# Layer 1 of the last sample: its 81 taps as diagonal matmuls in 64x64 tiles, in three lanes beside layer 2

## The chip, the core and the metric

The kernel runs on one core of a Trainium2 chip. The metric is the device time of one execution in microseconds (us), the median of several runs. Engines are named as in the profile: PE is TensorE (PEld its weight loads), DVE is VectorE, ACT is ScalarE, POOL is GpSimd, SP is the engine that only issues DMAs here.

## The reference: what is computed

Four layers with residuals work on x of shape (4, 256, 48, 48), fp32; each takes a group norm of x (32 groups) as its input.

```python
x = x + L0(gn(x))   # 8-head attention over all 2304 positions, then a 256x512 projection
x = x + L1(gn(x))   # a gate per channel: max pool, blur, 81-tap depthwise convolution, sigmoid
x = x + L2(gn(x))   # non-local block: attention with 64 channels, projection, batch norm
x = x + L3(gn(x))   # channel attention, 3x3 depthwise convolution, instance norm, leaky relu
```

Layer 1 is the one that is changed, for sample 3 alone:

```python
x_tem = blur_pool(max_pool_3x3(x), stride=3)               # 48x48 -> 16x16, per channel
x_h1 = dwconv(x_tem, w_h1, ((5, 5), (1, 1)))               # 11x3
x_w1 = dwconv(x_tem, w_v1, ((1, 1), (5, 5)))               # 3x11
x_h2 = inv_h(dwconv(h_transform(x_tem), w_h2, ...))        # 11x3 along a diagonal
x_w2 = inv_v(dwconv(v_transform(x_tem), w_v2, ...))        # 3x11 along the other
s = x_h1 + x_w1 + x_h2 + x_w2
gate = sigmoid((s - bn_mean) * bn_gamma / sqrt(bn_var + eps) + bn_beta)
return x * nearest_upsample(gate)
```

The four depthwise kernels fall on 81 different shifts of a 13x13 grid, so s is a sum of 81 shifted 16x16 images, each times one weight per channel.

## The kernel before: the parts that matter here

256 channels lie as two halves k = 0, 1 on 128 partitions. The main loop, `attend`, records attention in groups of two key blocks. In each group it issues the scores of this group, the pairwise sums for the softmax denominator of the group before, whatever else is due (`fills`), one step of the generators in `others`, and the value products of the group before. All engines run in program order (`manual_schedule`); only semaphores tie them together.

```python
for t, (u, g, st) in enumerate(groups):
    for j in range(g * G, (g + 1) * G):
        scores(u, j)                # 4 matmuls 64x64 tiles (fp32), then ACT: pt = exp(...)
    if prev is not None:
        add_up(*prev)               # POOL: half = pt0 + pt1;  DVE: acc += half
    do(due, t)
    do(fills, t)
    ...                             # lanes: next(gen) when due; a yielded number is the wait in groups
    if prev is not None:
        for j in ...: weigh(pu, j)  # value matmuls, 64x64 tiles
```

There are 16 phases of layer 0 (54 groups each) and then 4 phases of layer 2 (27 groups each). In layer 0 four of nine groups of a unit send their sum to POOL (`PAIRED`), in layer 2 of samples 0 to 2 all nine do. A query chunk ends with a total:

```python
def total(u):
    ab = [pj_tile()[:, :SL] for _ in range(2)]
    ...                                                # ones-matmuls over u["acc"]
    row = hpool.tile([P, 2, SL], F32, tag="half", name="row")   # hpool has 3 buffers
    for i in range(2):
        nc.scalar.copy(row[:, i, :], ab[i])
    ...                                                # l6 <- row by DMA, inverted, broadcast
```

Layer 1 of samples 0 to 2 runs beside layer 0 of the next sample. That of sample 3 runs beside layer 2 of samples 0 to 2, and the projection of sample 3 for layer 2 (`project2`) can only follow it. Its taps:

```python
def strips(b, k, norm, res):
    pd = lp.tile([P, 28, 28], F32, tag="pd", name="pd")
    nc.gpsimd.memset(pd, 0.0)
    blur = ...
    for half in range(2):
        ...                       # 12 ticks of DVE: maxima and blur of x, in tiles t1, t2, t3
    nc.scalar.activation(pd[:, 6:22, 6:22], blur, AF.Identity, bias=norm["nb"][...], scale=rs64)

    def products(n):              # 4 taps a round (5 in the first), 81 in all
        for i, t in enumerate(ROUNDS[n]):
            dr, dc = TAPS[t]
            nc.scalar.activation(
                bufs[n % 3][:, :, min(n, 1) + i].rearrange("p (r c) -> p r c", c=AS),
                pd[:, PAD + dr : PAD + dr + AS, PAD + dc : PAD + dc + AS],
                AF.Identity, scale=grid[:, k, g : g + 1],
            )
    ...
        nc.vector.tensor_reduce(to, bufs[n % 3][:, :, : min(n, 1) + len(taps)], AX.X, ALU.add)
```

and how sample 3 was placed:

```python
l1 = [l1_all(b) for b in range(B)]       # gn, strips 0, strips 1 with gated 0 aside, gated 1, gn
...
fns = project2(b + 1, norms2[b + 1], twos[b + 1])
if b + 2 == B:
    slots = list(range(n - 6, n))        # sample 3's projection: the last 6 groups of sample 2
spread(work, fns, slots)
...
others.append((part(l1[B - 1], ticks, b + 2 == B), ticks, first, end))
```

`gated` multiplies x by the gate (POOL, three strips of 128x768) and adds the constant part (DVE, three strips); `w_stats` multiplies a finished part of layer 2's result by W into two `pj` tiles and takes their statistics on DVE. All of `pj`'s users share two PSUM tiles.

Of the kernel before, what the change touches and what calls it, by code (L numbers as in the profile page):

```python
# [14 lines left out]
P = 128  # L15
# [59 lines left out]
def usual_path(  # L75
# [32 lines left out]
    load_x(0)  # L108
    vec = cpool.tile([P, 9, NK], F32, name="vec")
    nc.scalar.dma_start(vec, vecs)  # L110
    dw = cpool.tile([P, 4, NK, 33], F32, name="dw")
    nc.scalar.dma_start(dw, dww)

    wtp = thphi_w.rearrange("(k p) o -> p k o", p=P)
    w2c = cpool.tile([P, NK, 3, D], F32, name="w2c")
# [47 lines left out]
    def rsqrt(o, i):  # L163
        nc.gpsimd.tensor_tensor(o, i, mhalf[:, : i.shape[1]], ALU.pow)
# [5 lines left out]
    def gn(b, res, halves=range(NK)):  # L170

        if "st" not in res:
            res["st"] = small.tile([P, NK, NSL, 6], F32, tag="gn_st", name="gn_st")
        st = res["st"]
        for s in range(NSL):
            for k in halves:
                nc.vector.bn_stats(st[:, k, s, :], X[b][:, k, s * SL : (s + 1) * SL])
            yield 0
        mv = small.tile([P, NK, 2], F32, tag="gn_mv", name="gn_mv")
        for k in range(NK):  # L180
            nc.vector.bn_aggr(mv[:, k, :], st[:, k].rearrange("p s f -> p (s f)"))
        yield 3
        ps = pj_tile()
        nc.tensor.matmul(ps[:, 0:NK], lhsT=gmat, rhs=mv[:, :, 0], start=True, stop=True)
        gm = small.tile([P, NK], F32, tag="gn_gm", name="gn_gm")
        nc.vector.tensor_copy(gm, ps[:, 0:NK])
        dev = small.tile([P, NK], F32, tag="gn_dev", name="gn_dev")
        nc.vector.tensor_sub(dev, mv[:, :, 0], gm)
        sq = small.tile([P, NK], F32, tag="gn_sq", name="gn_sq")
        nc.vector.tensor_mul(sq, dev, dev)  # L190
        nc.vector.tensor_add(sq, sq, mv[:, :, 1])
        yield 2
        ps = pj_tile()
        nc.tensor.matmul(ps[:, 0:NK], lhsT=gmat, rhs=sq, start=True, stop=True)
        gv = small.tile([P, NK], F32, tag="gn_gv", name="gn_gv")
        nc.vector.tensor_scalar(gv, ps[:, 0:NK], GN_EPS, None, ALU.add)
        rs = small.tile([P, NK], F32, tag="gn_rs", name="gn_rs", bufs=6)
        rsqrt(rs, gv)
        yield 2
        nb = small.tile([P, NK], F32, tag="gn_nb", name="gn_nb", bufs=6)  # L200
        nc.vector.scalar_tensor_tensor(nb, gm, -1.0, rs, ALU.mult, ALU.mult)
        res["rs"], res["nb"] = rs, nb
        yield 1
# [82 lines left out]
    def total(u):  # L286

        ab = [pj_tile()[:, :SL] for _ in range(2)]
        for h, c in enumerate(HALVES):
            for r, out in zip(HALVES, ab):  # L290
                nc.tensor.matmul(  # L291
                    out[c], lhsT=ones[r], rhs=u["acc"][r, h, :], start=True, stop=True
                )
        row = hpool.tile([P, 2, SL], F32, tag="half", name="row")
        for i in range(2):
            nc.scalar.copy(row[:, i, :], ab[i])
        u["l6"] = small.tile([P, 2, LW], F32, tag="l6", name="l6")
        for c in HALVES:
            for i in range(2):
                nc.sync.dma_start(  # L300
                    u["l6"][c, i, :],
                    row[c.start : c.start + 1, i, :].rearrange("o (p w) -> o p w", w=LW),
                )

    def invert(u):
# [270 lines left out]
        }  # L576


    grid = lp.tile([P, NK, GRID * GRID], F32, name="grid")
    nc.gpsimd.memset(grid, 0.0)  # L580
    g2 = grid.rearrange("p k (r c) -> p k r c", r=GRID)
    for k in range(NK):
        wh1 = dw[:, 0, k, :].rearrange("p (a b) -> p a b", b=3)
        wv1 = dw[:, 1, k, :].rearrange("p (a b) -> p a b", b=11)
        wh2 = dw[:, 2, k, :].rearrange("p (a b) -> p a b", b=3)
        wv2 = dw[:, 3, k, :].rearrange("p (a b) -> p a b", b=11)
        s = g2[:, k, 1:12, 5:8]
        nc.gpsimd.tensor_add(s, s, wh1)
        s = g2[:, k, 5:8, 1:12]
        nc.gpsimd.tensor_add(s, s, wv1)  # L590

        s = grid[:, k, 23 : 23 + 132].rearrange("p (a t) -> p a t", t=12)[:, :, 0:3]
        nc.gpsimd.tensor_add(s, s, wh2)

        for a in range(3):
            s = grid[:, k, 11 + 13 * a : 11 + 13 * a + 132]
            s = s.rearrange("p (b t) -> p b t", t=12)[:, :, 0]
            nc.gpsimd.tensor_add(s, s, wv2[:, a, :])
    inv1 = lp.tile([P, NK], F32, name="inv1")
    v1 = lp.tile([P, NK], F32, name="v1")  # L600
    nc.vector.tensor_scalar(v1, vec[:, V_V1, :], BN_EPS, None, ALU.add)
    rsqrt(inv1, v1)
    nc.vector.tensor_mul(inv1, inv1, vec[:, V_G1, :])

    NT = 4
    ROUNDS = [range(0, NT + 1)] + [
# [3 lines left out]
    STRIP_TICKS = 2 * 6 + 2 + len(ROUNDS)  # L610
    GATE_TICKS = 7

    def strips(b, k, norm, res):

        xb = X[b][:, k, :].rearrange("p (r c) -> p r c", c=HW)
        pd = lp.tile([P, AS + 2 * PAD, AS + 2 * PAD], F32, tag="pd", name="pd")
        nc.gpsimd.memset(pd, 0.0)
        blur = lp.tile([P, AS, AS], F32, tag="blur", name="blur")
        for half in range(2):

            r0, nr = ((0, 25), (22, 26))[half]
# [40 lines left out]
            )  # L662
            yield half

        rs64 = lp.tile([P, 1], F32, tag="rs64", name="rs64")
        nc.vector.tensor_scalar(rs64, norm["rs"][:, k : k + 1], 1.0 / 64.0, None, ALU.mult)
        nc.scalar.activation(
            pd[:, PAD : PAD + AS, PAD : PAD + AS], blur, AF.Identity,
            bias=norm["nb"][:, k : k + 1], scale=rs64,
        )  # L670

        bufs = [
            lp.tile([P, L1_BUF], F32, tag=tag, name="prod").rearrange("p (n s) -> p n s", s=NT + 1)
# [3 lines left out]
        def products(n):  # L677
            for i, t in enumerate(ROUNDS[n]):
                dr, dc = TAPS[t]
                g = (dr + 6) * GRID + dc + 6  # L680
                nc.scalar.activation(  # L681
                    bufs[n % 3][:, :, min(n, 1) + i].rearrange("p (r c) -> p r c", c=AS),
                    pd[:, PAD + dr : PAD + dr + AS, PAD + dc : PAD + dc + AS],
                    AF.Identity, scale=grid[:, k, g : g + 1],
                )

        products(0)
# [3 lines left out]
        for n, taps in enumerate(ROUNDS):  # L691
            last = n == len(ROUNDS) - 1
            if n + 2 < len(ROUNDS):
                products(n + 2)
            to = bufs[(n + 1) % 3][:, :, 0]
            if last:
                res["acc"] = lp.tile([P, AS, AS], F32, tag="l1acc", name="l1acc")
                to = res["acc"].rearrange("p r c -> p (r c)")
            nc.vector.tensor_reduce(  # L699
                to, bufs[n % 3][:, :, : min(n, 1) + len(taps)], AX.X, ALU.add  # L700
            )
            yield 0

    def gated(b, k, norm, res):

# [169 lines left out]
    def l1_all(b):  # L875
# [20 lines left out]
        yield from gated(b, 1, norms1[b], one)  # L896
        yield from gn(b, norms2[b], [1])

    L1_ALL = 2 * GN_TICKS + NK * STRIP_TICKS + GATE_TICKS
    l1 = [l1_all(b) for b in range(B)]  # L900

    def part(gen, n, last):
        while n > 0 or last:
            wait = next(gen, None)
            if wait is None:
                return
            n -= 1
            yield wait

    def spread(work, fns, slots):  # L910

# [18 lines left out]
    for i, (b, p) in enumerate(order):  # L930
# [15 lines left out]
        if (b, p) == (2, 0):  # L946
            for s in range(NSL):
                work.setdefault(s, []).append(lambda s=s: send(s))
                work.setdefault(s + 8, []).append(lambda s=s: receive(s))
        if b > 0:  # L950
            ticks = -(-L1_ALL // NPAIR)
            first = AT_AFTER + 2 if p == 0 else 0
            others.append((part(l1[b - 1], ticks, p == NPAIR - 1), ticks, first, n - 2))
        if (b, p) == (B - 1, NPAIR - 1):
            others.append((part(l1[b], L1_AHEAD, False), L1_AHEAD, n - L1_AHEAD - 3, n))
        if p == 1 and b + 1 < B:
            others.append((gn(b + 1, norms0[b + 1]), GN_TICKS, 0, n - 2))
        phases.append(([l0_unit(b, p, c, pairs[b][p]) for c in range(NCH)], work, others))
# [2 lines left out]
    for b in range(B):  # L961
# [8 lines left out]
        if b + 1 < B:  # L970
            spread(work, stats(b, 0), [23, 24])
            fns = project2(b + 1, norms2[b + 1], twos[b + 1])
            slots = [s for s in range(n) if s % NG not in (2, 3, 4, 5, 6)]
            if b + 2 == B:
                slots = list(range(n - 6, n))
            spread(work, fns, slots)
            first, end = 4 if b == 0 else 0, n - 6 if b + 2 == B else n
            ticks = (L1_ALL - L1_AHEAD) * (end - first) // (3 * n - 6 - 4) + 1
            others.append((part(l1[B - 1], ticks, b + 2 == B), ticks, first, end))
        else:  # L980
            spread(work, stats(b, 0), [14, 15])
            spread(work, stats(b, 1), [23, 24])
            others.append((diagonals(), NK * len(PE_TAPS), 4, 22))
# [1232 lines left out]
```

## Time and profile before

| | before |
|---|---|
| median of 3 runs | 3762.78 us (3761.7 to 3763.52) |
| span of the profiled execution | 3765.1 us |
| scores, PE | 13,824 matmuls 64x384 in layer 0, 1,728 in layer 2 |
| exponentials, ACT | 1944, 814 ns each |
| pair sums `half`, POOL | 477, 1957 ns each |
| taps of layer 1, ACT | 648, 371.5 us in all four samples |
| reductions of taps, DVE | 152, 1480 ns each |

How to read it: an instruction stands as line, engine, operation, out<-in, shape and count; an fp32 matmul appears as two passes. The rows by stretch give for each engine the busy time and the number of instructions, then the granted share of the TensorE clock, the DMA share and GB/s. Layer 2's first scores with the tiles `qv`, `kd` start at 3014.9 us; the first tap of the last sample's layer 1 is at 3104.2 us, its last at 3304.0 us.

### The profile page before, as it was taken

Reading aid. Unit: us, or ns where it says so; the run is one execution under the profiler, and the core shown is the slowest. Engines: PE = TensorE matmul, PEld = TensorE weight load, DVE = VectorE, ACT = ScalarE, POOL = GpSimd, SP = SyncE. Lnnn points to the kernel's source line nnn. Section 1 sums busy time; section 2 is a strip of 40 time slices with the busy share of each in tenths; the row PEclk is TensorE's granted clock in tenths of the full one; section 3 lists DMA queues with packets and bytes.
Section 4 is the critical chain, followed back from the end, with each engine's and each line's share of the span. In section 5 each row is a group of like instructions: output and inputs, shape, how many; then the busy total and the mean of one; then the engine's idle time right before and its main releaser. Section 6 shows DMA issues by size and latency. Waiting matters only on the chain.

```text
span 3765.1 us, 85621 instructions
## 1 busy us (share of the span) xinstructions
PE 3547.9 (94%) x35954; PEld 1761.9 (47%) x35954; DVE 2544.2 (68%) x3199; ACT 2395.9 (64%) x3865; POOL 1354.2 (36%) x858
## 2 busy tenths in 40 slices
PE   7999999999999999999999999999999988789685
PEld 4454545555444445444444444444444543345343
DVE  2455545458778675587786756777867567866687
ACT  4656666565876875558768755587686548754353
POOL 1333333333334233333333433333333354564242
PEclk9999999999999999999999999999999998899897
DMA  3111111111111111311111111111111100000001
GB/s 134 25 25 21 26 22 25 21 27 18 28 17 25 21 29 16 79 16 29 16 29 16 29 16 30 15 29 17 29 12 25 18 4 6 5 6 6 26 30 72
DMA packets 114748, 97.84 MB, mean 26 GB/s; under 512 B 56384, under 2 KB 111792, under 8 KB 112560
## 3 DMA queue, kind: packets, MB, share of 16 engines
q1 hardware_dynamic: 111584, 91.14, 13.2%
q8 instruction: 283, 4.64, 0.5%
q10 hardware_dynamic: 2768, 1.14, 0.1%
q14 instruction: 113, 0.93, 0.1%
HBM read 59.33 MB, written 11.80 MB: 19 GB/s over the span
## 4 chain that ended last, share of the span: by engine, by line
PE 70%; DVE 18%; ACT 6%; issue 3%; POOL 2%; DMA 1%; DVEq 0%; SPq 0%; ACTq 0%; POOLq 0%
PE sc L238 26%; PE av L258 26%; DVE acc L284 6%; PE pj L499 6%; PE pj L556 4%; PE pj L513 3%; ACT prod L681 3%; DVE sc L1206 2%; PE pj L291 1%; ACT pt L244 1%; DVE av L1206 1%; PE pj L775 1%; DVE acc L278 1%; PE pj L803 1%; POOL half L269 1%
## 5 line engine op out<-in xcount | busy, mean ns | idle before, releaser
L244 ACT ACTIVATE pt<-sc 128x768 f32<-128x768 f32 x1944 | 1478.4, 814 | 947.0 <-PE sc L238 944.5
L269 POOL TENSOR_TENSOR half<-pt 128x768 f32<-128x768 f32 x477 | 933.2, 1957 | 1764.1 <-ACT pt L244 1656.9
L238 PE MATMUL sc<-q,k 64*64 64x384 f32 x13824 | 1290.2, 486 | 20.4 <-DVE q L544 11.2
L258 PE MATMUL av<-pt,v 64*64 64x384 f32 x13824 | 1291.7, 486 | 0.0
L284 DVE TENSOR_TENSOR acc<-acc,pt 128x768 f32<-128x768 f32 x792 | 863.9, 1091 | 105.8 <-ACT pt L244 24.3
L238 PEld LDWEIGHTS sc<-q,k 64*64 64x64 f32 x13824 | 521.8, 133 | 640.1 <-issue 514.0
L258 PEld LDWEIGHTS av<-pt,v 64*64 64x64 f32 x13824 | 524.1, 133 | 602.8 <-issue 567.2
L284 DVE TENSOR_TENSOR acc<-acc,half 128x768 f32<-128x768 f32 x459 | 480.0, 1046 | 289.7 <-POOL half L269 288.0
L560 DVE SCALAR_TENSOR_TENSOR x<-pj,bo,x 128x384 f32<-128x384 f32 x192 | 117.7, 617 | 409.7 <-PE pj L556 408.9
L681 ACT ACTIVATE prod<-pd,grid 128x256 f32<-128x256 f32 x648 | 371.5, 750 | 0.7 <-DVE prod L699 0.5
L499 PE MATMUL pj<-xs,w 128*128 128x384 f32 x768 | 265.2, 489 | 0.0
L699 DVE TENSOR_REDUCE prod<-prod 128x256 f32<-128x1280 f32 x152 | 224.9, 1480 | 29.6 <-ACT prod L681 29.1
L335 POOL TENSOR_TENSOR o<-o,rinv 128x384 f32<-128x384 f32 x95 | 117.8, 1240 | 344.7 <-DMA rinv<-rinv 331.6
L238 PE MATMUL sc<-qv,kd 64*64 64x384 f32 x1728 | 174.3, 508 | 40.3 <-ACT pt L244 40.2
L556 PE MATMUL pj<-o,wo 128*128 128x384 f32 x384 | 163.9, 525 | 21.6 <-DVE bias L466 10.9
L499 PEld LDWEIGHTS pj<-xs,w 128*128 128x128 f32 x768 | 139.2, 192 | 77.4 <-ACT v L518 4.8
L258 PE MATMUL av<-pt,qv 64*64 64x384 f32 x1728 | 175.1, 509 | 0.0
L513 PEld LDWEIGHTS pj<-w,xs 128*128 128x128 f32 x1152 | 137.5, 193 | 56.9 <-issue 50.9
L513 PE MATMUL pj<-w,xs 128*128 128x128 f32 x1152 | 155.0, 285 | 1.6 <-ACT w L468 1.6
L278 DVE TENSOR_TENSOR acc<-pt 128x768 f32<-128x768 f32 x99 | 122.5, 1237 | 24.3 <-ACT pt L244 24.3
L238 PEld LDWEIGHTS sc<-qv,kd 64*64 64x64 f32 x1728 | 72.3, 139 | 119.8 <-ACT pt L244 58.0
L327 ACT COPY raw<-av 128x768 f32<-128x768 f32 x108 | 86.2, 799 | 39.5 <-PE av L258 39.5
(216 smaller groups left out, 2547.1 us busy)
## 6 DMA issues: line engine op xcount, KB each, us to landing
xs<-in_x_dram SPq DMA_DIRECT2D x96, 384.0 KB
rinv<-rinv SPq DMA_DIRECT2D x208, 94.5 KB
x<-in_x_dram SPq DMA_DIRECT2D x6, 1152.0 KB
out_dram<-x SPq DMA_DIRECT2D x6, 1152.0 KB
l<-row SPq DMA_DIRECT2D x416, 1.5 KB
w<-in_wqkv_dram SPq DMA_DIRECT2D x32, 192.0 KB
rinv<-ls SPq DMA_DIRECT2D x208, 1.5 KB
x_out<-x SPq DMA_DIRECT2D x6, 384.0 KB
```

The lines of the kernel that those rows point to most:

```text
L238: nc.tensor.matmul(ps[c * D : (c + 1) * D, h, :SL], lhsT=u["of"]["k"][r, j0 : j0 + D], rhs=u["of"]["q"][r, u["qc"]], start=True, stop=True,)
L244: nc.scalar.activation(pt, ps[:, :, :SL], AF.Exp, scale=u["scale"])
L258: nc.tensor.matmul(u["av"][h * D : (h + 1) * D, half, :SL], lhsT=value(u, j, h)[r], rhs=pt[r, h, :], start=j == 0, stop=j == JB - 1,)
L269: nc.gpsimd.tensor_add(half, pts[0], pts[1])
L278: nc.vector.tensor_add(u["acc"], ready[0], ready[1])
L284: nc.vector.tensor_add(u["acc"], u["acc"], term)
L335: eng.tensor_mul(o, o, u["rinv"])
L499: nc.tensor.matmul(ps, lhsT=at["w"][:, k, t, :], rhs=xs[s][:, k, :], start=k == 0, stop=k == NK - 1,)
L513: nc.tensor.matmul(ps[:, i * P : (i + 1) * P], lhsT=xs[s][:, k, i * P : (i + 1) * P], rhs=at["w"][:, k, 2, :], start=k == 0, stop=k == NK - 1,
L556: nc.tensor.matmul(ps[:, :SL], lhsT=wo[:, p, k * P : (k + 1) * P], rhs=o, start=True, stop=True)
L681: nc.scalar.activation(bufs[n % 3][:, :, min(n, 1) + i].rearrange("p (r c) -> p r c", c=AS), pd[:, PAD + dr : PAD + dr + AS, PAD + dc : PA ...
L699: nc.vector.tensor_reduce(to, bufs[n % 3][:, :, : min(n, 1) + len(taps)], AX.X, ALU.add)
```

## The change

For sample 3, a tap becomes a matmul with a 64x64 diagonal of its weights, for each half of the partitions; the sum over taps is formed in PSUM. A round has 12 taps. Even and odd taps accumulate in different quarters of two PSUM tiles, so that all four 64x64 tiles of the array are in use, two taps at a time. GpSimd builds the diagonals, two rounds ahead; ScalarE copies each round's four quarters into the storage of `wo`, which layer 0 no longer needs; VectorE adds them. Maxima, taps and gates are three generators that advance side by side, at most one step a group each, and the projection of sample 3 follows, one function a group, as soon as the normalization is there. The weights of the taps lie in a compact table `wt`, built during the first phase of layer 0. In layer 2 the rows of `total` come from the pool `o`, which is idle then.

```diff
-    dw = cpool.tile([P, 4, NK, 33], F32, name="dw")
-    nc.scalar.dma_start(dw, dww)
...
+        if "shift" in u["of"]:
+            rows = [op.tile([P, SL], F32, tag="o", name="row") for _ in ab]
...
-                    AF.Identity, scale=grid[:, k, g : g + 1],
+                    AF.Identity, scale=wt[:, k, t : t + 1],
...
+    TAPS_AT_ONCE = 12
+
+    def strips_pe(b, k, norm, res):
...
+        def build(n):
+            taps = rounds[n]
+            xs = xsp.tile([P, NK, SL], F32, tag="xs", name="diag1")
...
+            nc.gpsimd.tensor_tensor(
+                diag[n], ident2.unsqueeze(1).to_broadcast([P, len(taps), D]),
+                wt[:, k, taps[0] : taps[-1] + 1].unsqueeze(2).to_broadcast([P, len(taps), D]),
+                ALU.mult,
+            )
+
+        def product(n):
+            taps = rounds[n]
+            ps = [pj_tile()[:, : AS * AS] for _ in HALVES]
+            runs = [taps[0::2], taps[1::2]]
+            for i in range(len(runs[0])):
+                for h, r in enumerate(HALVES):
+                    for e, run in enumerate(runs):
...
+                        nc.tensor.matmul(
+                            ps[h][HALVES[h ^ e]].rearrange("p (r c) -> p r c", c=AS),
+                            lhsT=diag[n][r, run[i] - taps[0], :],
+                            rhs=pd[r, PAD + dr : PAD + dr + AS, PAD + dc : PAD + dc + AS],
+                            start=i == 0, stop=i == len(run) - 1,
+                        )
+            for h, r in enumerate(HALVES):
+                for e in range(2):
+                    nc.scalar.copy(
+                        parts[r, n % 2, e].rearrange("p r c -> p (r c)"), ps[h][HALVES[h ^ e]]
+                    )
+
+        def add(n):
+            two = parts[:, n % 2]
+            if n == 0:
+                nc.vector.tensor_add(acc, two[:, 0], two[:, 1])
+                return
+            for e in range(2):
+                nc.vector.tensor_add(acc, acc, two[:, e])
...
+    def l1_last(b, ahead):
...
+        return [ahead, tops(), sums(), gates()]
...
-            if b + 2 == B:
-                slots = list(range(n - 6, n))
-            spread(work, fns, slots)
-            first, end = 4 if b == 0 else 0, n - 6 if b + 2 == B else n
-            ticks = (L1_ALL - L1_AHEAD) * (end - first) // (3 * n - 6 - 4) + 1
-            others.append((part(l1[B - 1], ticks, b + 2 == B), ticks, first, end))
+            if b + 2 < B:
+                spread(work, fns, slots)
+            for gen in lanes:
+                others.append((pace(gen), 1000, 4 if b == 0 else 0, n + 1))
+            if b + 2 == B:
+                others.append((follow(fns, norms2[b + 1]), 1000, 0, n))
```

## The prediction

> **What bounds the kernel now.** I read the page's busy shares and slices first, then cut the part that the change touches into stages, then looked at single instructions.
>
> ```profile
> PE 3547.9 (94%) x35954; PEld 1761.9 (47%) x35954; DVE 2544.2 (68%) x3199; ACT 2395.9 (64%) x3865; POOL 1354.2 (36%) x858
> ...
> PE   7999999999999999999999999999999988789685
> ...
> PEclk9999999999999999999999999999999998899897
> ```
>
> TensorE is the bound at 94%, and its row has holes only at the end: slices 33 to 36 (8, 8, 7, 8; a slice is 94 us). That is layer 2 of samples 0 to 2, where the last sample's layer 1 runs. I call one step of the main loop (two score tiles, two value tiles) a group; sample 3's layer 2 must wait for the last of 81 such groups. Cut by stages (first column the stretch, then busy us of each engine):
>
> ```profile
> 3015.90:3036.70 20.80, 18.79 (x184) 8.79 (x180) 11.66 (x17) 8.84 (x15) 8.19 (x5) 1.00 0.00 1
> 3036.70:3106.80 70.10, 61.45 (x632) 30.26 (x624) 52.55 (x61) 34.93 (x54) 40.51 (x22) 0.97 0.04 4
> 3106.80:3174.60 67.80, 54.57 (x516) 23.74 (x520) 45.65 (x41) 63.52 (x116) 27.39 (x17) 0.83 0.05 4
> 3174.60:3247.10 72.50, 60.66 (x556) 29.58 (x552) 64.54 (x72) 34.43 (x56) 44.87 (x24) 0.91 0.08 7
> 3247.10:3304.50 57.40, 44.51 (x456) 18.68 (x452) 42.99 (x39) 57.37 (x104) 25.03 (x15) 0.88 0.06 5
> 3304.50:3361.00 56.50, 47.07 (x544) 23.57 (x536) 49.17 (x53) 28.42 (x41) 47.11 (x26) 0.97 0.10 8
> 3361.00:3408.50 47.50, 44.78 (x356) 26.75 (x360) 15.20 (x18) 16.76 (x32) 14.26 (x9) 0.89 0.06 5
> ```
>
> Row by row (columns PE, PEld, DVE, ACT, POOL): start; maxima and blur of channel half 0; its tap products; maxima of half 1 with the gate of half 0; products of half 1; gate of half 1 and statistics; projection of sample 3, crowded into the last 6 groups. In the two product stages ScalarE is the bound (63.5 of 67.8, 57.4 of 57.4 us). In the two maxima stages it is VectorE and GpSimd together:
>
> ```profile
> 3067.48 2.48 POOL L269 TENSOR_TENSOR half<-pt 128x768 f32<-128x768 f32 x1 [0.19 <-ACT pt L244]
> ...
> 3068.20 3.00 DVE L627 TENSOR_TENSOR t<-x 128x1175 f32<-128x1175 f32 x1
> 3071.12 1.80 DVE L628 COPY t<-x 128x25 f32<-128x25 f32 x1
> ...
> 3082.12 1.42 DVE L627 TENSOR_TENSOR t<-x 128x1222 f32<-128x1222 f32 x1
> 3083.46 0.18 DVE L628 COPY t<-x 128x26 f32<-128x26 f32 x1
> ```
>
> A column copy takes 0.18 us while GpSimd is idle and 1.80 us behind a `half` sum; the maximum takes 1.42 or 3.00. The two take turns. So I add both: a group costs 1.81 (a `half` alone) + 0.95 (an `acc` alone) = 2.76 us there, against 2.58 us of TensorE (two stretches of 2.58 us had PE busy throughout). For groups 4 to 19: 16 x 2.76 = 44.2; maxima and blur 18.6 (their unblocked durations); fold, divide and shift of one result 3.8; clearing `pd` 0.7; small ones 2.5; sum 69.8 us. Measured: 70.1. I trust this sum below.
>
> [...] besides the rows above, the tap reduction took 1.48 us at 3108.05 with a `half` of 1.83 us started at 3108.39 beside it. [...] Scores and values agree: four start within 20 ns, the next four 322 ns after the first. [...] The new products sit between 64x64 scores and 64x64 values, so no change of mode is added.
>
> **The change, part by part.**
>
> *Removed.* 162 tap activations, and 40 reductions:
>
> ```profile
> L681 ACT ACTIVATE prod<-pd,grid 128x256 f32<-128x256 f32 x162 | 90.1, 747 | 0.3 <-DVE prod L699 0.3
> L699 DVE TENSOR_REDUCE prod<-prod 128x256 f32<-128x1280 f32 x38 | 56.3, 1481 | 29.6 <-ACT prod L681 29.1
> ```
>
> That is 90 us of ScalarE and 40 x 1.48 = 59 us of VectorE. TensorE lost, in the product stages, 67.8 - 54.6 + 57.4 - 44.5 = 26 us of idle time. The groups there would have taken about 47 and 37 us (13 x 2.58 and 12 x 2.58, plus the projections, totals and statistics among them), so the whole prize is about 125 - 84 = 41 us.
>
> *Added on TensorE.* Each tap is 2 channel halves x 2 passes (an fp32 matmul stands as two in the trace) = 4 quarter-tile passes, all four at once: 322 ns x 256/384 columns = 215 ns. 81 x 2 x 0.215 = 35 us, with a start per round (14 rounds x 0.2) 38 us.
>
> *Added on GpSimd.* 14 diagonals of 128x768 or less: 1.6 us like the fastest gate product (L726, also with a broadcast input) to 1.81 like a `half`: 24 us. *On VectorE*: 27 adds of 128x256, a third of an `acc`: 0.32 x 27 = 9 us. [...] *On ScalarE*: 56 copies of 64x256 from PSUM; a 128x192 copy took 0.32 us, so about 0.37: 21 us, hidden.
>
> *Moved.* Three lanes: the maxima of half 1 run beside the products of half 0. By the instruction order of the two programs, products stand in groups 19 to 25 and 34 to 41, and sample 3's projection is spread over groups 62 to 79 instead of 75 to 80. The row of the softmax total takes another pool, so that it holds none of the three `half` buffers. The tap table is built on GpSimd beside the first pair of layer 0 instead of at the start, where the first statistics wait for x until 11.48 us anyway: 0 to 0.5 us.
>
> *The sum.* TensorE's need: 332 busy now, of which some 13 are matmuls at a lowered clock (granted 0.91 over the stretch) = 319, plus 38 = 357 us. That alone would save 392.6 - 357 = 36 us. But stage by stage the later of the two needs counts:
> 1. Groups 0 to 3: 20.8, unchanged.
> 2. Group 4 to `pd` of half 0 (ScalarE stands still until blur is there): lock 12 x 2.76 + maxima 18.6 + two diagonals 3.6 + 6 others = 61; TensorE 50. Before, the same sum for the 14 groups up to `pd` gives 64 where the trace has 66.9 (3036.7 to 3103.6), so 63 here.
> 3. To `pd` of half 1: lock 15 x 2.76 = 41.4, maxima 18.6, 7 diagonals 12.7, 14 adds 4.5, gate of half 0 10, two folds 7.6, rest 2.7 = 97.5; TensorE 15 groups with 7 rounds 77. So 98.
> 4. Products of half 1: TensorE 9 x 2.58 + 7 rounds 18 + projections 8 + waits for PSUM tiles 5 = 54; lock about the same. 54.
> 5. Gate, statistics, to the normalization of sample 3: lock 18 x 2.76 + 11 + 7.6 + 2 = 70, and two groups for the chain of small steps: 76.
> 6. Projection spread: TensorE 19 x 2.58 + 28 + 6 = 83.
>
> Sum 394.8 against 392.6: +2, less 0.4 at the start and about 0.5 for the freed buffers. **Predicted: 3764 us.** The 41 us from ScalarE are nearly all given back: 38 to TensorE, the rest to the lock.
>
> **Rivals.** (a) *TensorE is the only bound.* For it: 94% busy, and layer 0 keeps it at 9 tenths with the same layer-1 work beside it. It gives 357 plus some 10 of waits, a time near 3737. Against it: the 69.8 and 70.1 us above; in layer 0 only 4 of 9 sums go to GpSimd, in layer 2 all 9. (b) *Waits for PSUM tiles.* A round takes both `pj` tiles, which projection, totals and statistics also use; where they meet (groups 19, 21, 23 to 25, 34, 35, 37, 39, 41) the round waits for an eviction by ScalarE or by a VectorE that lags. I count 11 us for ten meetings; if VectorE lags 3 us each time it is 30, a time near 3785. (c) *Nothing moves*, because sample 3 waits for something else: the stage rows speak against it, as TensorE works 44.8 of 47.5 us as soon as the normalization is there.
>
> **Range and chances.** The terms of stages 2, 3 and 5 are good to 5% each, about 12 us; the lock could be milder for adds of 256 columns (-10), meetings worse (+15). So 3747 to 3784. Two per cent are 75 us: a gain of that size exceeds all idle time of the stretch, and a loss of it would need every round to stall by 5 us. Whether it ends above or below 3762.78 is nearly even, slightly toward slower.
>
> **What would show it.** Right: the diagonal matmuls stand at about 2.6 us a round of 48 passes; ScalarE's busy time in the stretch falls from 244 to about 175 us; `acc` rows lengthen beyond today's 1.5 us mean; TensorE idles mostly in groups 10 to 18 and 26 to 33, ended by blur or statistics of VectorE; the stretch stays within 380 to 415 us. Wrong: `acc` and the maxima run beside the diagonals undisturbed and TensorE is above 95% there (then rival a), or rounds start late behind `pj` (rival b), or a round takes 4 us and more because weight loads don't hide.

## The result, and the profile after

The changed kernel took 3754.45 us (median of 4 runs, 3745.72 to 3755.02) against 3763.15 us for the kernel before: ratio 0.9972, 95% interval 0.9955 to 0.9989. On another chip (the run `change_again` below) it took 3749.06 us, ratio 0.9964 (0.995 to 0.9977). So it gains 9 to 13 us, some 0.3%. The predicted time, 3764 us, was on the wrong side of the kernel before; the predicted range holds the result.

First the page of the changed kernel: busy time of each engine, then tenths of busy time in 40 slices.

```profile
PE 3569.4 (95%) x36602; PEld 1787.1 (48%) x36602; DVE 2502.2 (67%) x3185; ACT 2335.0 (62%) x3759; POOL 1398.7 (37%) x890
...
PE   7999999999999999999999999999999998999685
...
PEclk9999999999999999999999999999999999999897
```

The holes in slices 33 to 36 (8, 8, 7, 8 before) are closed but for one 8, and the granted clock there is back at 9. ScalarE lost 61 us of work, GpSimd gained 44.5.

The same stretch by stages, cut at the events that the prediction named, with the whole stretch in the last row (columns: stretch, length, then busy us and instructions of PE, PEld, DVE, ACT, POOL, granted clock, DMA share, GB/s):

```profile
3013.80:3034.60 20.80, 18.79 (x184) 8.79 (x180) 11.66 (x17) 8.84 (x15) 9.03 (x6) 1.00 0.00 1
3034.60:3088.90 54.30, 53.53 (x552) 25.78 (x544) 53.78 (x59) 26.55 (x40) 42.23 (x19) 1.00 0.05 5
3088.90:3172.60 83.70, 73.01 (x909) 47.70 (x912) 64.02 (x73) 40.89 (x77) 55.21 (x30) 0.98 0.04 4
3172.60:3233.90 61.30, 57.54 (x679) 39.05 (x681) 34.91 (x41) 28.28 (x56) 33.88 (x20) 0.94 0.05 5
3233.90:3312.40 78.50, 72.48 (x764) 36.23 (x760) 52.14 (x60) 37.39 (x55) 54.22 (x30) 0.96 0.09 8
3312.40:3396.40 84.00, 78.94 (x804) 38.32 (x800) 29.08 (x35) 39.99 (x63) 42.17 (x26) 1.00 0.08 8
3013.80:3396.40 382.60, 354.28 (x3872) 195.87 (x3868) 245.58 (x281) 181.93 (x304) 236.75 (x128) 0.98 0.06 6
```

And the whole stretch of the kernel before:

```profile
3015.90:3408.50 392.60, 331.84 (x3224) 161.36 (x3220) 281.76 (x296) 244.26 (x410) 207.35 (x116) 0.91 0.06 5
```

Subtract the PE column from the length: TensorE idled 60.8 us before and 28.3 us after. It got 22.4 us more to do and lost 32.5 us of idle time; the stretch is 10.0 us shorter. The added matmuls are more than 22.4 us (14 rounds of 2.67 us are 37): part of them is paid back by the old ones, fewer of which run at a lowered clock (granted 0.91 before, 0.98 after). An example of matmuls that run slower after a long stop stands below.

What the idle time was, before and after. First one wait of the kernel before (engine, tile and line, what it waited for, total us, times, longest), then groups of the changed kernel from 3005 us to the end of this stretch (count | busy us, mean ns | idle before, and what ended it):

```profile
PE sc L238 <- ACT pt L244: 40.2, 11, 9.5
```

```profile
L267 POOL TENSOR_TENSOR half<-pt 128x768 f32<-128x768 f32 x83 | 174.4, 2106 | 117.3 <-ACT pt L242 103.5 <-DVE lmin L324 5.5 <-DVE acc L282 4.8
L236 PE MATMUL sc<-qv,kd 64*64 64x384 f32 x1304 | 128.0, 485 | 1.3 <-ACT pt L242 1.3
L282 DVE TENSOR_TENSOR acc<-acc,half 128x768 f32<-128x768 f32 x64 | 76.7, 1199 | 49.7 <-POOL half L267 49.1
...
L794 DVE TENSOR_TENSOR l1acc<-l1acc,wo 128x256 f32<-128x256 f32 x24 | 25.5, 1063 | 11.0 <-ACT wo L784 9.8
L760 POOL TENSOR_TENSOR diag<-ident,wt 128x768 f32<-128x768 f32 x12 | 21.2, 1763 | 23.4 <-PE pj L776 22.5 <-DVE acc L276 0.9
```

Scores waited 40.2 us for exponentials that stood behind taps on ScalarE; now 1.3 us. So the wait that the change was made for is gone. What remains was mostly there before: 20.4 of the old 60.8 us stood before matmuls into one of the two `pj` tiles, and 27 of the 28.3 us do now. Rounds of taps account for 4.2 of the 27, in five stops; 2.5 are waits for data of the group norm, the rest mostly waits for a tile. The longest, on TensorE and then on VectorE in the same microseconds (start, us, engine, line, operation, count, and in brackets the idle time before it):

```profile
3164.72 1.47 PE L236 MATMUL sc<-qv,kd 64*64 64x384 f32 x16
3172.05 2.02 PE L944 MATMUL pj<-y,Ww 64*64 64x384 f32 x8 [5.85 <-DVE bst L952]
3173.38 3.24 PE L256 MATMUL av<-pt,qv 64*64 64x384 f32 x16
```

```profile
3163.51 1.75 DVE L826 RECIPROCAL gate<-gate 128x256 f32<-128x256 f32 x1
...
3166.83 1.69 DVE L683 TENSOR_TENSOR tf<-tf 128x128 f32<-128x128 f32 x1
3168.44 1.89 DVE L684 TENSOR_TENSOR tf<-tf 128x128 f32<-128x128 f32 x1
...
3171.43 1.03 DVE L952 BATCH_NORM_STATS2 bst<-pj 128x6 f32<-128x384 f32 x2
```

`w_stats` puts two products into `pj` and needs both tiles again for the next pair. Their statistics stand in VectorE's program order behind the gate of half 0 and the blur of half 1, so TensorE stops for 5.85 us. Two additions of 128x128 take 1.69 and 1.89 us there, with a gate product and a `half` on GpSimd beside them; one at 3128.77 us, with nothing on GpSimd beside it, takes 0.28. After the stop the 16 value passes take 3.24 instead of 1.47 us: the granted clock is 0.60 from 3172.05 to 3178 us, and 1.00 from 3158.92 to 3166. ScalarE stands still at this place too: the instruction that writes `pd` of half 1 waits 8.64 us for the same blur, and the next exponentials come behind it.

### The profile page after: what moved, and what is told of

It reads as the page before. It is cut to its first block, busy times and chain, and to the rows that moved or that the text cites. A ratio compares the mean times of both kernels' runs of the same rounds, so it can differ in the third digit from the quotient of the medians.

```text
span 3752.6 us, 86878 instructions
## 1 busy us (share of the span) xinstructions
PE 3569.4 (95%) x36602; PEld 1787.1 (48%) x36602; DVE 2502.2 (67%) x3185; ACT 2335.0 (62%) x3759; POOL 1398.7 (37%) x890
## 4 chain that ended last, share of the span: by engine, by line
PE 73%; DVE 16%; issue 4%; ACT 4%; POOL 2%; DMA 1%; DVEq 0%; SPq 0%; ACTq 0%; POOLq 0%
PE sc L236 27%; PE av L256 27%; PE pj L501 6%; DVE acc L282 5%; PE pj L558 4%; PE pj L515 3%; DVE sc L1372 2%; ACT prod L716 1%; POOL half L267 1%; PE pj L289 1%; DVE av L1372 1%; ACT pt L242 1%; PE pj L776 1%; PE pj L886 1%; DVE acc L276 1%
## 5 line engine op out<-in xcount | busy, mean ns | idle before, releaser
L267 POOL TENSOR_TENSOR half<-pt 128x768 f32<-128x768 f32 x477 | 945.6, 1983 | 1699.0 <-ACT pt L242 1613.9
L236 PE MATMUL sc<-q,k 64*64 64x384 f32 x13824 | 1290.9, 487 | 22.1 <-DVE q L546 12.5
L282 DVE TENSOR_TENSOR acc<-acc,pt 128x768 f32<-128x768 f32 x792 | 870.5, 1099 | 106.0 <-ACT pt L242 24.4
L282 DVE TENSOR_TENSOR acc<-acc,half 128x768 f32<-128x768 f32 x459 | 460.3, 1003 | 328.3 <-POOL half L267 327.5
L716 ACT ACTIVATE prod<-pd,wt 128x256 f32<-128x256 f32 x486 | 281.5, 752 | 0.4 <-DVE prod L734 0.2
L734 DVE TENSOR_REDUCE prod<-prod 128x256 f32<-128x1280 f32 x114 | 168.6, 1479 | 0.0
```

The lines of the kernel that those rows point to most:

```text
L236: nc.tensor.matmul(ps[c * D : (c + 1) * D, h, :SL], lhsT=u["of"]["k"][r, j0 : j0 + D], rhs=u["of"]["q"][r, u["qc"]], start=True, stop=True,)
L267: nc.gpsimd.tensor_add(half, pts[0], pts[1])
L282: nc.vector.tensor_add(u["acc"], u["acc"], term)
L716: nc.scalar.activation(bufs[n % 3][:, :, min(n, 1) + i].rearrange("p (r c) -> p r c", c=AS), pd[:, PAD + dr : PAD + dr + AS, PAD + dc : PA ...
```

## The experiments

The table has all runs, times in us. The ratio is to runs of the kernel before on the same chip. "Stretch" is the length of the same stretch in each trace, "PE busy" is TensorE in it, "idle" the difference; where a kernel was traced twice, both are given.

| kernel | median | ratio to before (95%) | stretch | PE busy | idle |
|---|---|---|---|---|---|
| before | 3763.15 | 1 | 392.6 | 331.8 | 60.8 |
| before_again | 3761.57 | 0.9996 (0.999 to 1.0003) | 389.0 | 327.4 | 61.6 |
| the change | 3754.45 | 0.9972 (0.9955 to 0.9989) | 382.6 | 354.3 | 28.3 |
| change_again | 3749.06 | 0.9964 (0.995 to 0.9977) | 382.7 | 354.4 | 28.3 |
| e1_lanes_scalar_taps | 3753.48 | 0.9976 (0.9968 to 0.9984) | 390.1 | 330.9 | 59.2 |
| lanes_scalar_taps_again | 3755.05 | 0.9975 (0.9965 to 0.9986) | 387.2 | 327.8 | 59.4 |
| e2_serial_pe_taps | 3761.93 | 1.0 (0.9991 to 1.0009) | 393.1 | 354.5 | 38.6 |
| e3_two_of_twelve | 3733.24 | 0.9922 (0.9906 to 0.9939) | 364.4 | 325.7 | 38.7 |
| e6_crowded_projection | 3741.96 | 0.9948 (0.9931 to 0.9965) | 376.5 | 350.5 | 26.0 |
| e7_statistics_moved | 3733.87 | 0.9923 (0.9908 to 0.9938) | 365.8 | 347.1 | 18.7 |
| e8_half_sums_on_vector | 3738.73 | 0.9942 (0.9927 to 0.9957) | 371.6 | 350.4 | 21.2 |
| e9_rows_in_half_pool | 3753.28 | 0.9974 (0.9964 to 0.9984) | 385.6 | 355.6 | 30.0 |
| e10_best_of_both | 3727.26 | 0.9909 (0.9893 to 0.9926) | 360.0 | 345.6 | 14.4 |
| e11_no_half_sums | 3726.32 | 0.9904 (0.9888 to 0.9921) | 360.4 | 345.5 | 14.9 |

**The theories.** *Turns*: as predicted, VectorE and GpSimd in turns set the length (the prediction's "lock": their durations added up). *TensorE*: its work sets the length, and what is left is waits for `pj`.

### Half of the change: the lanes, with the taps left on ScalarE

```diff
-                yield from strips_pe(b, k, norm, res[k])
+                yield from strips_act(b, k, norm, res[k])   # 2 taps a round: ACT products, DVE tensor_reduce
```

> The three lanes and the spread projection stay; the taps go back to ScalarE (162 activations, reductions on VectorE, 3 taps then 2 a round, 8 taps a group), in buffers that are free here. Theory A, the gain comes from the placement in lanes and the move to TensorE is neutral (about 41 us of idle time traded for 37 us of matmuls plus waits): 3735 to 3757 us. Theory B, the gain comes from relieving ScalarE: back to 3762 us or more, with ScalarE busy throughout the tap groups.

```profile
3008.72:3398.77 390.05, 330.89 (x3224) 153.17 (x3220) 289.24 (x336) 236.91 (x410) 211.04 (x115) 0.93 0.06 5
```

```profile
PE sc L236 <- ACT pt L242: 35.1, 15, 5.7
```

The three lanes alone leave TensorE idle as long as before, 59.2 us: scores still wait 35.1 us for ScalarE (second fence, the waits). In the stretch they are worth 2.5 us, although the median, 3753.48 us, lies where theory A put it.

### The other half: the taps on TensorE, one generator as before

```diff
-            for gen in lanes:
-                others.append((pace(gen), 1000, 4 if b == 0 else 0, n + 1))
+            others.append((part(l1[B - 1], ticks, b + 2 == B), ticks, first, end))   # maxima, taps, gate in series
```

> The taps stay on TensorE; the three lanes are undone: statistics, maxima, taps and gate of the last sample follow one another in one generator as before the change, with the projection in the last 6 groups again. Theory A: 3760 us or more, the gain is gone. Theory B: 3754 us as with the change, or within 3 us of it.

```profile
3009.49:3402.54 393.05, 354.46 (x3872) 207.70 (x3868) 253.71 (x282) 182.75 (x305) 240.19 (x130) 0.97 0.06 6
```

```profile
PE pj L944 <- DVE bst L952: 22.2, 3, 12.4
```

All 648 new passes stand there (3872 against 3224), and the scores' wait is gone, but TensorE idles 38.6 us, 22.2 of it behind late statistics (second fence). The median, 3761.93 us, is that of theory A. A reservation: with fewer steps, the evenly paced generator also reaches the first `pd` at 106.0 us after the start of the stretch (87.7 before, 75.1 in the change), so this is not a perfectly clean half. Nor is the place of the projection shared out evenly: the first half keeps it spread, this one crowds it again, and spreading it alone costs 6 us (below). Neither half shortens the stretch much (2.5 us and none); together they do, by 10.0.

### Both kernels once more

e1's median had gained 9.5 us although its stretch had gained 2.5, so it and the kernel before were run again.

> The kernel before once more, for a second trace of it. If the stretch of layer 2 with the last sample's layer 1 in it is steady from run to run, it lasts 392.6 us again, to within 0.5 us, and only the point at which layer 0 ends differs from 3015.9 us (anywhere from 3005 to 3016). If the first trace was an outlier, the stretch differs by several us, and what the other kernels gained in it has to be counted again.

> The three lanes with the taps left on ScalarE once more. Its first trace had the stretch at 390.05 us, 2.5 us under the kernel before, but its median was 9.5 us lower. If lanes alone gain little and the rest lies in layer 0, whose instructions are the same: stretch 390 us again, ratio anywhere from 0.997 to 1.0. If the lanes are the whole gain and the first trace was an unlucky execution: stretch near 383 us, ratio 0.9975 again.

The second trace of before has a stretch of 389.0 us, not 392.6 to within 0.5: the idle time is the same (61.6 us), the matmuls beside it were 4.5 us shorter. Over both traces, lanes alone shorten the stretch by 2.2 us (390.8 to 388.6), the whole change by 8.2 (to 382.65). The ratio of lanes alone repeats, 0.9975. The rest of its gain, then, lies outside the stretch; the last section shows where a part of it is.

### A sixth of the matmuls

This kernel leaves out 67 of the 81 taps in each half (it keeps the first two of each round), so its output lacks them.

```diff
-            runs = [taps[0::2], taps[1::2]]
+            runs = [taps[0:1], taps[1:2]]
```

> The change with only the first two taps of each round multiplied: 14 of 81 taps a half are kept and the others are left out of the sum, so the output is not the reference's; diagonals, copies and adds stay. Takes 14 rounds x about 2.2 us = 30 us of matmuls from TensorE. If TensorE is the bound in all tap groups: 3724 us. If VectorE and GpSimd[...] bound the taps of half 0 and TensorE only those of half 1: about 15 us less, near 3740 us.

```profile
3009.33:3373.74 364.41, 325.74 (x3336) 169.05 (x3332) 253.66 (x281) 181.42 (x304) 240.22 (x128) 0.97 0.06 6
```

TensorE had 28.5 us less to do and the stretch became 18.2 us shorter, with ScalarE busy as long as in the change, VectorE and GpSimd 8 and 3 us longer. If the turns had set the length, nothing would have been gained; if TensorE alone had, 28.5. The gain lies between: about two thirds of the matmul time are on the path. The rest became waiting: TensorE idles 38.7 instead of 28.3 us, and one stop alone, before a round that waits for statistics on VectorE, grew from 0.75 to 7.39 us.

### The projection of sample 3 crowded again

```diff
-                others.append((follow(fns, norms2[b + 1]), 1000, 0, n))
+                others.append((follow(fns, norms2[b + 1]), 1000, n - 6, n))   # and three functions a group
```

> The change with the projection of sample 3 in the last 6 groups again (three functions a group), all else as it is. If spreading it matters because TensorE then works where VectorE and GpSimd set the pace: 8 to 12 us slower than the change, near 3764 us. If it only moves work: within 3 us, near 3755 us.

Neither expectation held. Spread out, the projection had looked harmless; crowded into the last groups, it made the kernel faster: the stretch went from 382.7 to 376.5 us. From the normalization on, it takes 78.9 us in place of 84.0: 2.8 us less idle time and 2.3 us less TensorE time. The idle time: stops of 0.67 to 0.77 us stand wherever one projection meets another user of `pj` in a group, six in the last stage of the change, two here. The TensorE time: a group without projection lasts 2.58 us, with one 4.18 to 4.23, with three 6.85 to 6.95 (groups without a stop), so a projection costs 1.60 to 1.65 us alone and at most 1.46 in a row of three. Projections use 128x128 or 128x64 tiles between blocks of 64x64; what makes one alone dearer no run shows. This part of the change costs time.

### The statistics moved to where VectorE is not late

This is the kernel above with the `w_stats` of the finished parts of samples 0 to 2 in other groups, away from the gates and the blur.

```diff
-        if b > 0:
+        if b == 1:
+            spread(work, stats(0, 0), [15, 20])
+        if b == 2:
+            spread(work, stats(0, 1), [0, 1])
...                                        # (0,2) 2, 7; (1,0) 8, 9; (1,1) 10, 11; (1,2) 13, 14
+        if b == 3:
...
```

> As the kernel with the crowded projection, and the eight matrix products with W whose statistics VectorE takes are moved from groups 23, 24, 32, 33, 41, 42, 50, 51, 59, 60, 68, 69 to groups 42, 47, 54 to 56, 61 to 65, 67, 68, where VectorE idles. If TensorE's long stops (group 32 takes 10.7 us and group 52 takes 11.7 us where about 3.3 and 4.3 would do) come from these products waiting behind a late VectorE: 10 to 15 us less than the crowded one. If they come from VectorE and GpSimd being the bound in sum there: no gain, the stops move to the exponentials.

```profile
3010.85:3376.65 365.80, 347.06 (x3872) 196.44 (x3868) 256.22 (x282) 182.03 (x304) 240.74 (x129) 0.99 0.06 6
```

Same instructions, another place (twelve calls of `w_stats`, not eight): the stretch is 10.7 us shorter than in the kernel above. TensorE idles 18.7 instead of 26.0 us, and its busy time falls by 3.5 us, with a granted clock of 0.99 instead of 0.98. So waits for `pj` behind a late VectorE were on the path. But the longest stop, 5.84 us in the kernel above, is still there. It moved to the scores, as the second theory said, since `pd` of half 1 waits for the blur on VectorE, and the exponentials stand behind `pd` on ScalarE:

```profile
3165.91 2.84 PE L236 MATMUL sc<-qv,kd 64*64 64x384 f32 x16 [6.17 <-ACT pt L242]
```

```profile
3164.56 0.61 ACT L697 ACTIVATE pd<-blur,gn_nb,rs 128x256 f32<-128x256 f32 x1 [7.69 <-DVE rs L696]
```

### Fewer half sums on GpSimd

In layer 2 of samples 0 to 2, four of nine pair sums go to GpSimd instead of all nine; for the rest VectorE adds both tiles itself.

```diff
-            "paired": PAIRED if b == B - 1 else range(NG),
+            "paired": PAIRED,
```

> The change with only four of nine groups of a query chunk summed on GpSimd in layer 2 of samples 0 to 2, as layer 0 does it; the other five go to VectorE as two adds each. [...]VectorE's busy time rises by some 40 us. If the sum of VectorE and GpSimd bounds the maxima and gate stages: 5 to 12 us less than the change. If VectorE's own queue does: 5 to 15 us more.

```profile
3005.50:3377.10 371.60, 350.44 (x3872) 194.66 (x3868) 255.34 (x327) 182.18 (x304) 147.21 (x85) 0.99 0.06 6
```

```profile
L794 DVE TENSOR_TENSOR l1acc<-l1acc,wo 128x256 f32<-128x256 f32 x24 | 17.2, 716 | 11.8 <-ACT wo L784 10.6
```

VectorE has 46 instructions more, 44 us at 0.95 each, yet is busy only 9.8 us longer: the others became shorter (the tap additions fell from 1063 to 716 ns). The stretch lost 11.1 us, as the first expectation said. This speaks for the turns with GpSimd as what makes VectorE late: in the change, the ten tap additions with nothing on GpSimd beside them take 0.42 to 0.43 us, the fourteen others 0.69 to 2.04. That VectorE waits less for `half` (49.1 us for 64 sums in the change, 35.1 us for 36 here) may add to it, and the run doesn't part the two.

### The rows of the softmax total back in the pool of `half`

```diff
-        if "shift" in u["of"]:
-            rows = [op.tile([P, SL], F32, tag="o", name="row") for _ in ab]
-        else:
+        if True:
             row = hpool.tile([P, 2, SL], F32, tag="half", name="row")
```

> The change with one part undone: the rows of the softmax total are again in the pool of the half sums, one of three buffers. If the freed buffer mattered: 2 to 6 us more than the change. If not: within 1.5 us.

The stretch is 2.9 us longer (385.6), nearly all of it one stop before the group norm's matmul that grew from 0.77 to 3.39 us. The small part is worth about 3 us, within the first expectation and more than the 0.5 predicted.

### The best of both, and no half sums at all

The first is the moved statistics with four of nine sums on GpSimd; the second has none of them on GpSimd in samples 0 to 2.

```diff
-            "paired": PAIRED if b == B - 1 else range(NG),
+            "paired": PAIRED,                               # e10
+            "paired": PAIRED if b == B - 1 else (),         # e11
```

> Crowded projection, statistics moved and four of nine half sums on GpSimd, together. The stretch from the first layer-2 group to sample 3's layer 2 took 382.7 us with the change, 365.8 with the statistics moved (crowded included) and 371.6 with the half sums on VectorE. If the two gains add (16.9 + 11.1): 355 us, a time near 3723 us. If TensorE is the bound by then: about 360 us, near 3728 us.

> As the one before, but with no half sum on GpSimd at all in layer 2 of samples 0 to 2: VectorE adds every tile of exponentials, 1.74 us a group, GpSimd keeps diagonals, gates and results. If only the sum of the two engines counts: as fast as the one before or up to 5 us faster. If VectorE's own queue becomes the bound: 5 to 15 us slower than it.

```profile
3009.62:3369.60 359.98, 345.57 (x3872) 198.32 (x3868) 256.02 (x327) 182.24 (x305) 143.46 (x85) 0.99 0.06 6
```

3727.26 us, ratio 0.9909 (0.9893 to 0.9926): faster than both kernels. Of the 11.1 us of the sums 5.8 remain, since TensorE now idles only 14.4 us; the second expectation, 360 and 3728 us, held. Nearly half of the 14.4 us is the stop before the scores, 6.84 us here. Without any half sum the time is the same (3726.32) and that stop still 5.43 us, so from here on the half sums on GpSimd no longer cost time.

## Why the prediction was right and wrong

**Right.** *A round* takes 2.67 us (a bare group with one lasts 5.24 to 5.28 us, one without 2.58); 14 of them are 37 us, predicted 38 (the 0.2 us for a start was an estimate; beyond 12 taps of 0.215 a round takes 0.09). *Copies*: 367 ns each, predicted 0.37. *Diagonals*: 1763 ns, predicted 1.6 to 1.81. *ScalarE* 181.9 us, predicted about 175. *The stretch* lies within 380 to 415 us. Stages 1, 5 and 6 came out at 20.8, 78.5 and 84.0 us (predicted 20.8, 76, 83). That the range held the time is partly luck: stages 2 and 3 were put 23 us too long, the other four 11 us too short in sum, so that nearly half of the error cancelled.

**Wrong: the turns as a sum of durations, in stages 2 and 3.** "I trust this sum" is the sentence that failed. Stage 2 took 54.3 us where it gave 63, stage 3 took 83.7 where it gave 98: 23 us too many. The sum had been backed by 69.8 against 70.1 us in the kernel before. The first 30.6 us of that row, taken alone, show that the agreement was accidental:

```profile
3036.70:3067.30 30.60, 30.60 (x324) 15.31 (x320) 16.53 (x19) 16.61 (x25) 17.47 (x10) 1.00 0.01 2
```

TensorE was busy for all of it and VectorE for 16.5 us. The maxima had not begun, because one generator does group norm and maxima in series. Only the rest was VectorE's. Eight of the 16 groups lie in each part, so the sum gives 8 x 2.76 = 22.1 us for the first, where 30.6 passed, and 47.7 us for the second, where 39.5 did. It left out VectorE's idle time in the one, was too long in the other, and the two errors cancelled. In the lanes the first maximum runs beside the group norm, at 3035.43 us, and stage 2 fits into 54.3 us with both engines nearly full (53.53 us PE, 53.78 DVE). As TensorE idles 0.8 us there, the turns can cost no more than that in this stage. In stage 3 neither is full (73.01 and 64.02 of 83.7 us). The durations also overcount: an `acc` of 0.95 us begun at 3085.12 us in the trace of before is followed by the next instruction at 3085.99, 0.08 us before the end of its record. The prediction's TensorE need for these stages (50 and 77 us) was closer to what happened: 53.5 busy and 73.0.

**Wrong: stage 4.** 61.3 us instead of 54, and not by the waits for `pj`: they were put at 5 us and TensorE idled 3.8. Its own work took 57.5 us where the other terms give 49. The sum left out `w_stats` and a total (4.0 and 1.3 us), and it took the clock as full (granted 0.94), while the matmuls behind the 5.85 us stop ran slowly (granted 0.60).

**Wrong: single sizes.** The tap additions were put at 0.32 us each: the shortest is 0.42, the mean 1.06, 25.5 us for 24 of them against 9 for all. The `acc` rows were to lengthen beyond 1.5 us; they shortened to 1.2 us, and the `half` rows took the wait instead (2106 ns against 2002 in the same stretch before). The lowered clock was put at 13 us of TensorE's 332. With e10 as the measure, whose clock is nearly full (granted 0.99), the work of before is by estimate about 345.6 - 37 = 308 us, so the lowered clock cost some 24 us (19 in its second trace). TensorE's need after the change is thus near 346, not 357. Idle time was to lie mostly in groups 10 to 18 and 26 to 33; about 9 of the 28.3 us do.

**The rivals.** Rival (a), TensorE, was nearer than the sum: TensorE was busy 354 us against its 357. It fails only in allowing 10 us for waits; there are 28. Rival (b) counted 11 us of waits of the rounds for `pj` tiles, up to 30 with a late VectorE; the rounds waited 4.2 us. Most of the 27 us before matmuls into `pj` belong to users that the change did not add. So the changed stretch is TensorE's work plus stops, most of them for `pj`. The turns are not a bound of their own there; they add to VectorE's lateness, which reaches TensorE through the `pj` tiles and, behind the blur, through ScalarE (the stop that e7 and e10 keep). The two thirds of e3, the gains of e6 and e7 by placement alone, and e8 together carry this. How much of the lateness is the turns and how much VectorE's own queue no run parts.

## What to carry to other kernels

A sum of durations that agrees with one measured stage is not yet a bound: cut the stage in halves and see whether the engines summed up are really busy in each. Moving work to a less loaded engine and reordering the work around it can each be worth little alone in a stage and pay together (here -2, +2 and -8 us, against the mean of the two traces of before). When an engine shares a few PSUM tiles, place each producer where the reader of the previous result is not late in its own program order; here that was worth 10.7 us of the stretch, the whole change 8 to 10. And look where the lateness goes next: the longest stop only moved to another wait.

## What the runs showed that was not expected

**Layer 0 changed too, where only the order on GpSimd differs.** In both traces of before, the three phases with the blur of samples 0 to 2 (phases 4, 8 and 12, counted from 0) take 186.7, 187.7 and 188.0 us (the first 186.8 in the second trace); in the twelve traces of kernels with the change or parts of it they take 184.1 to 185.6, 183.3 to 185.7 and 184.2 to 185.7. In phase 8 nearly all of it is one group: 14.45 us before, 9.90 to 12.48 in the others. TensorE there, in the kernel before:

```profile
1684.09 2.90 PE L556 MATMUL pj<-o,wo 128*128 128x384 f32 x4 [2.24 <-DVE bias L466]
1686.92 2.79 PE L258 MATMUL av<-pt,v 64*64 64x384 f32 x16
```

and in `change_again`:

```profile
1679.90 1.53 PE L558 MATMUL pj<-o,wo 128*128 128x384 f32 x4 [0.43 <-DVE bias L468]
1681.36 1.52 PE L256 MATMUL av<-pt,v 64*64 64x384 f32 x16
```

A 128x3 copy, `bias`, stands on VectorE behind three additions and a scaled one; a `half` of 2.52 us (1678.74 us) and a product of 1.48 us (1681.23 us) run on GpSimd beside them in before, and the first addition of 128x400 takes 2.31 us, where the same one takes 0.71 us with GpSimd idle (3079.38 us). TensorE stands still for 2.24 us until `bias` comes, and the matmuls after it take 2.90 and 2.79 us instead of 1.53 and 1.52, at a granted clock of 0.51 (1684.09 to 1689.60 us). So a stop of 2.24 us costs 2.64 us more in slower matmuls here, where one of 0.43 us costs nothing. Stops of 1.12 to 1.29 us stand at this place in 31 of the 36 phases of the twelve traces: behind 17 of them matmuls ran slowly, behind 14 they didn't. In the first trace of the change, the clock granted over some 3 us after such stops is 1.00, 1.00 and 0.68 (1.18, 1.26 and 1.24 us, at 938.34, 1683.13 and 2428.01 us), and in before a stop of 0.70 us (1873.49 us) has matmuls of 2.55 and 2.14 us behind it. So the length of the stop alone does not tell. Ahead of each of these stops stand 12 matmuls of one column that take 1.40 us; what part they have in it no run shows.

Where VectorE falls behind, the traces show. From phase 1 on the instructions are the same, and so is their order on PE, VectorE and ScalarE. On GpSimd one moved: the change splits `strips`, and the clearing of `pd` went from ahead of the maxima to behind the blur, from group 31 to group 47 of these phases. In before, a column copy of VectorE waits at group 31 for a `half` (2.87 us) and then the clearing as well:

```profile
1627.68 2.48 DVE L628 COPY t<-x 128x25 f32<-128x25 f32 x1
1629.38 0.75 POOL L617 MEMSET pd<- 128x784 f32 x1
```

and in `change_again` for the `half` alone:

```profile
1625.30 1.81 DVE L654 COPY t<-x 128x25 f32<-128x25 f32 x1
```

The copy takes 2.48 to 2.49 us in these phases in both traces of before and 1.80 to 1.81 in all twelve others. In before VectorE stays behind from there, and `bias` stands 0.9 to 2 us later in its phase than in the others. No run moves the clearing alone, so this cause is read from the traces and not tested. Other phases got longer (phase 15 by 0.4 to 1.4 us), and layer 0 as a whole, from its first exponential, went from 2959.5 and 2959.1 us to between 2951.1 and 2958.0. As all kernels with parts of the change have this too, it explains part of the gain of the lanes alone outside the stretch, not all of it.
